# A grouped convolution with two ways of splitting its images: nine of eleven images combined and two by plain taps, instead of three of five combined and two by rows

## The chip, the core and the metric

The kernel runs on one core of one Trainium2 chip. The metric is the device time of one execution in microseconds (us). The core's engines work side by side, each through its own queue in program order: PE (TensorE, matmuls), DVE (VectorE), ACT (ScalarE), POOL (GpSimd), and SP (SyncE), which issues most of the DMA transfers here. They wait for one another by semaphores.

## What is computed

160 images of 128 channels and 32 x 32 pixels are normalised in groups of four channels, convolved 3 x 3 with one of five quantised weight sets, and added to the input:

```python
x = x + _L0_conv_ref(_gn(x), L0_conv_U)

# _gn: per image and group of 4 channels
((g - m) / sqrt(s + eps))

# _L0_conv_ref: U in two quantised parts, then a grouped convolution with N = 5 groups
v1 = s1 * floor(U / s1)
v2 = s2 * floor((U - v1) / s2)
w  = (v1 + v2).reshape(128 * 5, 128, 3, 3)
act = conv(x.reshape(32, 5 * 128, 32, 32), w, stride 1, padding 1, groups 5)
```

Channels lie on the 128 partitions, so one tap of the convolution is a matmul of a 128 x 128 weight matrix with the shifted pixels of an image. The kernel takes the images in an order in which 32 successive ones share a weight set.

## The kernel before

**Numbers in two halves.** [...] each normalised image is split into a high part (the value rounded to 16 bits) and a low part (what is left), and both are multiplied.

**Three ways to do an image.** The two rows of a pair of output rows can share work: with sums and differences of neighbouring lines, the nine taps need fewer products, at the price of additions on DVE.

- *Combined* (`combined(i)` true): high and low parts are both made from sums and differences. `beside_pairs` (POOL, lines 678 and 708) and `combine` (DVE, lines 690 and 697) make the tile `v` of 2048 columns from the raw image; `high_combined` (ACT, line 738) makes `vh`, and `low_combined` (DVE, line 744) makes `vl`. PE does 24 matmuls.
- *By rows* (`combined(i)` false, from image 3 on): the high part `hi` goes through the 18 plain taps (line 788; nine taps, even and odd output rows apart). `low_part` (DVE, line 751) makes the low part, and `combinations` (DVE, lines 764, 772 and 773) makes the tile `rows` of its sums and differences, which PE takes in 12 matmuls (line 843). In all 30. The normalised image `z` comes from POOL (line 714), or from ACT (line 640) where an image is the first of its statistics group (`by_scalar_too`); `hi` comes from ACT (line 648).
- *Plain*: both parts through the taps, 36 matmuls. Only the first three images are done so.

Before the change the pattern is: up to image 6 by rows, then every other image combined, from `FIFTHS` = 30 to `THIRDS` = 130 three of five combined, and then three of four.

**What PE does for an image.** A combined or by-rows image has two products that even and odd output rows share. `sums_of_pairs(i)` puts them in the banks `m2` (one for all images) and `m1a` or `m1b` (by parity of i). ACT copies m2 out (`leave(i)`, line 891), and DVE writes half sum and half difference into the two output banks `eo` of the image (`pairs(i)`, lines 903 and 905). Then `main(i)` adds the rest of the products into these banks. There are two pairs of `eo` banks. When an image is done, ACT copies it out (`residual`, line 929), and POOL issues a DMA that adds it to the output (line 953), where SP has stored the input already (line 968).

**Order.** The order of every queue is the program's own (`tc.manual_schedule()`); nothing reorders it. In iteration i of the main loop, PE does `sums_of_pairs(i + 1)` and then `main(i)`. DVE does, in this order: the low part of image i + 3; a step of the next weight set; `pairs(i + 1)`; in some iterations a scale of the statistics (line 307); `combine(i + 5)`; another weight step; in some iterations five small statistics operations (lines 296 to 302). ACT does: the sum over an image to be measured (line 241, image i + 15); the copy of image i - 1; `leave(i + 1)`; the high part of image i + 4; the squares over the measured image (line 248). POOL does its part of image i + 5 once DVE has come to the low part of the iteration, and then the DMA of image i - 1.

**Weight steps.** A weight set is quantised on DVE and ACT while the set before it is in use. The class `Later` hands out its steps at a pace of 36 over the 25 or so images that remain; `later.take(1)` issues one step if one is due, and two or three places in an iteration ask for one.

**Buffers.** Two images share a chunk of the input. A pool of `CHUNKS` = 11 holds them; after the start, a chunk is loaded (line 497) in the iteration that `consumed` gives for the chunk that lay `CHUNKS` before it. The tiles `vh` rotate through `wide_parts`, with 4 buffers.

Of the kernel before, what the change touches and what calls it, by code (L numbers as in the profile page):

```python
# [10 lines left out]
MM = mybir.dt.float16  # L11
ALU = mybir.AluOpType
# [24 lines left out]
class Later:  # L37
# [25 lines left out]
    def finish(self):  # L63
        run(self.steps)
# [110 lines left out]
def last_of(steps, last=None):  # L175
    for last in steps:
        pass
    return last
# [207 lines left out]
class Main:  # L386
# [24 lines left out]
    STAT_LEAD = 15  # L411
    FURTHER = 11
    LOAD_LEAD = 18
    CHUNKS = 11
    STEADY = 7
    BY_VECTOR = (8, 10, 11, 14, 19, 24, 29, 34)
    FIFTHS = 30
# [10 lines left out]
    def __init__(self, tc, ctx, keep, x, u, out):  # L428
        self.tc = tc
        nc = self.nc = tc.nc  # L430
        self.imgs, C, self.H, self.W = x.shape
        P = self.P = nc.NUM_PARTITIONS
        assert C == P and self.H * self.W == 1024
        self.per_set = self.imgs // N_SETS
        self.xv = x.rearrange("(b n) c h w -> n c b (h w)", n=N_SETS)
        self.ov = out.rearrange("(b n) c h w -> n c b (h w)", n=N_SETS)
        self.uv = u.rearrange("n (o i k) -> n o i k", o=C, k=TAPS)

        def pool(name, bufs, **kw):
            return ctx.enter_context(tc.tile_pool(name=name, bufs=bufs, **kw))  # L440

        self.const = pool("const", 1)
        self.qpool = pool("quant", 1)
        self.wpool = pool("weights", 2)
        self.upool = pool("u", 1)
        self.xpool = pool("x", self.CHUNKS)
        self.zpool = pool("z", 2)
        self.parts = pool("parts", 4)
        self.rows = pool("rows", 5)
        self.wide = pool("wide", 2)  # L450
        self.wide_parts = pool("wide_parts", 4)
        self.evac = pool("evac", 2)
        self.sums = pool("sums", 3)
        self.unread = pool("unread", 1)
        self.small = pool("small", 3)
        self.ps_eo = pool("ps_eo", 2, space=PSUM)
        ps_m = pool("ps_m", 1, space=PSUM)
        ps_small = pool("ps_small", 1, space=PSUM)
        self.steps = Steps(nc, keep)

        self.m1a, self.m1b, self.m2_ps = (
            ps_m.tile([P, self.H // 2, self.W], F32, tag=name, name=name)
            for name in ("m1a", "m1b", "m2")
        )
        self.pair = [self.m1a, self.m2_ps]

        small = ps_small.tile([P, 512], F32, tag="small", name="small")
        self.pt, self.pg = small[:, : ROW * P].rearrange("p (k o) -> p k o", k=ROW), small[:, ROW * P :]
        self.chunks, self.z, self.hi, self.v, self.eo, self.m2 = {}, {}, {}, {}, {}, {}
        self.sum, self.stored = {}, {}  # L470
        self.tables, self.wts, self.across = {}, {}, {}
        self.columns = []

        cuts = [0, 2, 4, 8, 12, 16, 20, *range(24, self.imgs + 1, 8)]
        self.groups = [range(a, b) for a, b in zip(cuts, cuts[1:])]
        self.group_of = {i: k for k, g in enumerate(self.groups) for i in g}
        self.stats = {}
# [173 lines left out]
    def combined(self, i):  # L651

        if i < self.STEADY or i >= self.imgs:
            return False

        if i < self.FIFTHS:
            return i % 2 == 1
        return i % 5 % 2 == 0 if i < self.THIRDS else i % 4 != 2

    def by_scalar_too(self, i):  # L660

# [39 lines left out]
    def beside_pairs(self, i, after):  # L701

        nc = self.nc
        if self.combined(i):
            self.v[i] = self.wide.tile([self.P, 2048], F32, tag="v", name=f"v{i}")
            self.after(self.outer_columns(i), after)
            even, odd = (self.image(i)[:, a::2] for a in range(2))
            ins = nc.gpsimd.tensor_sub(self.v[i][:, 1536:], odd, even)  # L708
        elif self.by_scalar_too(i):
            return  # L710
        else:
            st, j = self.column_of(i)
            z = self.z[i] = self.zpool.tile([self.P, 1024], F32, tag="z", name=f"z{i}")
            ins = nc.gpsimd.tensor_scalar(  # L714
                z, self.image(i), st.ngm[:, j], st.rstd[:, j], ALU.add, ALU.mult
            )
        self.after(ins, after)

    def last_but_one(self, last):
# [28 lines left out]

    def low_part(self, i):
        lo = self.los[i % len(self.los)]  # L750
        self.nc.vector.tensor_sub(  # L751
            lo[:, 1 : self.H + 1, :].rearrange("p h w -> p (h w)"),
            self.z.pop(i),
            self.hi[i].rearrange("p h w -> p (h w)"),
        )
        return lo

    def combinations(self, i):

# [15 lines left out]
    def taps(self, i, part, col, target, parities=(0, 1)):  # L775


        nc, H, W = self.nc, self.H, self.W
        tile, top = part
        n, _ = self.place(i)  # L780
        dw = col - 1
        c0, c1 = max(0, -dw), W - max(0, dw)
        for k in self.KS:
            for a in parities:

                first, end = int(a + k == 0), H // 2 - int(a + k == 3)
                s0 = 2 * first + a + k - 1 + top
                nc.tensor.matmul(  # L788
                    self.bank(target, a)[:, first:end, c0:c1],
                    self.wts[n, col][:, k, :],  # L790
                    tile[:, s0 : s0 + 2 * (end - first) - 1 : 2, c0 + dw : c1 + dw],
                    start=(i < self.FIRST and col == self.COLS[0] and k == 1 and top == 0),
                    stop=False,
                    skip_group_check=True,
                )
# [66 lines left out]
    def conv(self, i, on_the_way):  # L862


        if self.FIRST < i < self.imgs - 1:
            self.sums_of_pairs(i + 1)
        if i == self.FIRST:
            self.main(i, 0)
            self.sums_of_pairs(i + 1)
            on_the_way(self.COLS[1])  # L870
            self.main(i, 1)
            on_the_way(self.COLS[2])
        else:
            self.main(i, 0, lambda: on_the_way(self.COLS[1]))
            self.main(i, 1, lambda: on_the_way(self.COLS[2]))
        del self.v[i]

    def main(self, i, a, between=lambda: None):

        to = self.bank(self.eo[i], a)  # L880
        for step in self.KS:
            if step == self.KS[1] and a == 1 or step == self.KS[2] and a == 0:
                between()
            if not self.combined(i):
                self.taps(i, (self.hi[i], 0), step, self.eo[i], (a,))
            self.product(to, i, a, step, 2 * a)

    def leave(self, i):

# [93 lines left out]
    def run(self):  # L983
        nc, P = self.nc, self.P
# [33 lines left out]
        for k in range(4):  # L1018
            lo = self.const.tile([P, self.H + 2, self.W], MM, tag=f"lo{k}", name=f"lo{k}")
# [95 lines left out]
        for i in range(self.imgs):  # L1115
# [15 lines left out]
            if i < self.FIRST:  # L1131
# [3 lines left out]
                j = (i - 1) % self.FIRST  # L1135
# [10 lines left out]
            else:  # L1146
                j = i - 1
# [35 lines left out]
            else:  # L1183

                last = None
                for k in self.step_of(i, 2):
                    if self.combined(k):
                        last = last_of(self.low_combined(k), last)
                    else:
                        self.low_part(k)  # L1190
                        later.take(1)
                        last = last_of(self.combinations(k), last)
                last = later.take(1, last)
                if last:
                    before = self.last_but_one(last)
# [8 lines left out]
                if i > self.FIRST and not self.by_hand(j):  # L1204
                    self.residual(j)
                    self.accumulate(j)
                if i + 1 < self.imgs:
                    self.leave(i + 1)
                for st in ready:
                    if not st.late:  # L1210
# [1 line left out]
                for k in self.step_of(i, 3):  # L1212
                    if self.combined(k):
                        self.high_combined(k)
                        continue
                    if self.by_scalar_too(k):
                        self.normalise(k)
                    self.high_part(k)
                for k in by_scalar:
                    self.measure(k, (1,))  # L1220
            for st in middle:
# [12 lines left out]

            if i >= self.FIRST:

                if i + 1 < self.imgs:
                    self.pairs(i + 1)
                for st in scaled:
                    st.scales_by_vector()  # L1240
                for k in self.step_of(i, 4):
                    if self.combined(k):
                        self.combine(k)
                    later.take(1)
                later.take_scalar()
                if b in (self.per_set - 4, self.per_set - 2):
                    later.finish()
                for st in ready:
                    if st.late:
                        st.deviations_by_vector()  # L1250
# [65 lines left out]
```

## Time and profile before

| | |
|---|---|
| median of 3 runs | 967.39 us (966.81 to 967.67) |
| the profiled execution | 964.56 us |
| its span, first to last instruction | 962.5 us |
| PE busy | 927.8 us, 96% of the span, 4432 matmuls |
| DVE busy | 902.6 us, 94%, 1269 instructions |
| ACT busy | 862.7 us, 90%, 1167 instructions |
| POOL busy | 460.1 us, 48%, 477 instructions |
| DMA | 254.22 MB, mean 264 GB/s |
| granted clock of PE | 0.995 |

Each engine has its own row, and the rows overlap in time. A busy time is a sum over all stages of the kernel, so it does not tell by itself which engine sets the end. In the lines of a timeline the first number is the start in us from the span's beginning, the second the duration. In the rows of the stretches each engine has its busy time and, in brackets, its instructions. In the rows of waits the numbers are us in total, times, and the longest. Successive matmuls overlap: one lasts about 0.37 us from its start to its end, but the next one starts after some 0.21 us.

### The profile page before, as it was taken

The page shows a single profiled execution, that of the slowest core. Times are in us where ns is not written, and L with a number is a line of the kernel's source. Part 1 is how long each engine was busy: PE and PEld are TensorE (multiplying, and loading weights), DVE is VectorE, ACT ScalarE, POOL GpSimd, SP SyncE. Part 2 cuts the span into 40 slices and gives each one's busy share as a digit, 9 for nine tenths or more (in the row PEclk, how much of TensorE's full clock was granted, in tenths as well). Part 3 has the DMA queues.
Part 4 walks back from the last instruction along what each step waited for, and adds up shares of the span by engine and source line. Part 5 has one row for each costly group of instructions (what it writes and reads, how often), then busy time and mean ns, then how long its engine had stood idle before and what let it go on. Part 6 is the DMA issues. An engine that isn't in the chain of part 4 may idle for free.

```text
span 962.5 us, 13034 instructions
## 1 busy us (share of the span) xinstructions
PE 927.8 (96%) x4432; PEld 433.8 (45%) x4432; DVE 902.6 (94%) x1269; ACT 862.7 (90%) x1167; POOL 460.1 (48%) x477
## 2 busy tenths in 40 slices
PE   2899989999999999999999999999999999999997
PEld 1344434444444444444444444444444444444443
DVE  7989999999899999989999999899999998999993
ACT  5879989999899999999999999999999999997660
POOL 4344434456445445554545445545444366565640
PEclk9999999999999999999999999999999999999999
DMA  9079999999999999999999999999999999856563
GB/s 349 36 267 345 334 348 320 325 321 325 328 321 323 317 295 308 272 306 254 295 251 289 284 293 297 282 277 286 267 273 267 282 279 269 172 91 107 91 107 112
DMA packets 67450, 254.22 MB, mean 264 GB/s; under 512 B 5296, under 2 KB 5296, under 8 KB 67376
## 3 DMA queue, kind: packets, MB, share of 16 engines
q1 hardware_dynamic: 45344, 173.09, 48.0%
q0 software_dynamic: 22032, 80.23, 44.4%
q8 instruction: 36, 0.59, 0.2%
q14 instruction: 38, 0.31, 0.1%
HBM read 89.19 MB, written 164.10 MB: 263 GB/s over the span
## 4 chain that ended last, share of the span: by engine, by line


## 5 line engine op out<-in xcount | busy, mean ns | idle before, releaser
L788 PE MATMUL eo<-hi,wt 128*128 128x496 f16 (+3 forms) x1170 | 310.8, 376 | 2.4 <-DVE eo L905 1.7
L843 PEld LDWEIGHTS <-wt 128*128 128x128 f16 x1884 | 183.9, 99 | 211.5 <-DVE eo L905 2.7
L744 DVE SCALAR_TENSOR_TENSOR vl<-v,rstd,vh 128x2048 f16<-128x2048 f32 x94 | 221.8, 2360 | 0.2 <-ACT vh L738 0.2
L843 PE MATMUL eo<-vh,wt 128*128 128x512 f16 x561 | 210.1, 375 | 1.2 <-DVE eo L905 1.2
L843 PE MATMUL eo<-vl,wt 128*128 128x512 f16 x561 | 210.1, 374 | 0.0
L738 ACT ACTIVATE vh<-v,rstd 128x2048 f16<-128x2048 f32 x94 | 188.2, 2002 | 4.8 <-DVE v L697 4.3
L929 ACT COPY sum<-eo 128x1024 f32<-128x1024 f32 x153 | 161.0, 1052 | 32.3 <-PE eo L843 31.7
L788 PEld LDWEIGHTS <-wt 128*128 128x128 f16 x1242 | 121.2, 99 | 142.8 <-DVE eo L905 4.9
L678 POOL TENSOR_SCALAR v<-xt,ngm 128x64 f32<-128x64 f32 x94 | 79.1, 842 | 202.0 <-DVE vl L744 86.9
L248 ACT ACTIVATE junk<-xt,mv 128x1024 uint8<-128x1024 f32 x152 | 174.4, 1148 | 0.3
L241 ACT ACTIVATE junk<-xt 128x1024 uint8<-128x1024 f32 x152 | 160.5, 1056 | 13.3 <-DMA xt<-in_x_dram 10.0
L714 POOL TENSOR_SCALAR z<-xt,ngm,rstd 128x1024 f32<-128x1024 f32 x49 | 93.3, 1904 | 165.1 <-DVE rows L773 55.0
L843 PEld LDWEIGHTS <-across 128*128 128x128 f16 x1128 | 110.8, 98 | 131.9 <-issue 4.9
L843 PE MATMUL eo<-rows,wt 128*128 128x512 f16 x378 | 143.5, 380 | 0.0
L953 POOL DMA_DIRECT2D out_dram<-sum x153 | 133.7, 874 | 14.4 <-ACT sum L929 6.6
L690 DVE TENSOR_TENSOR v<-xt 128x960 f32<-128x960 f32 x94 | 114.0, 1212 | 0.0
L843 PE MATMUL m<-vl,across 128*128 128x496 f16 (+1 forms) x282 | 106.4, 377 | 2.1 <-DVE vl L744 2.1
L891 ACT ACTIVATE m<-m 128x512 f32<-128x512 f32 x157 | 93.7, 597 | 14.1 <-PE m L843 13.7
L843 PE MATMUL m<-vh,across 128*128 128x496 f16 (+1 forms) x282 | 106.2, 376 | 0.2 <-ACT m L891 0.2
L708 POOL TENSOR_TENSOR v<-xt 128x512 f32<-128x512 f32 x94 | 97.2, 1034 | 0.0
L751 DVE TENSOR_TENSOR lo<-z,hi 128x1024 f16<-128x1024 f32 x66 | 80.6, 1221 | 0.0
L286 POOL TENSOR_TENSOR rstd<-ve,mhalf 128x8 f32<-128x8 f32 (+2 forms) x24 | 42.3, 1761 | 65.1 <-DVE rows L773 21.1
(150 smaller groups left out, 1166.3 us busy)
## 6 DMA issues: line engine op xcount, KB each, us to landing
xt<-in_x_dram SPq DMA_DIRECT2D x78, 1024.0 KB, 9.6
out_dram<-sum POOLq DMA_DIRECT2D x153, 512.0 KB, 8.7
out_dram<-xt SPq DMA_DIRECT2D x76, 1024.0 KB, 14.2
out_dram<-xt SPq DMA_DIRECT2D x7, 512.0 KB, 3.3
u<-in_L_conv_U_dram SPq DMA_DIRECT2D x4, 576.0 KB, 13.6
xt<-in_x_dram SPq DMA_DIRECT2D x4, 512.0 KB, 10.1
range<-in_L_conv_U_dram SPq DMA_DIRECT2D x3, 576.0 KB, 8.3
u<-in_L_conv_U_dram SPq DMA_DIRECT2D x2, 288.0 KB, 3.1
```

Source lines behind the costliest of these rows:

```text
L241: self.nc.scalar.activation(junk, image, ACTF.Copy, scale=-1.0 / image.shape[1], accum_out=self.mv[:, j, 0:1],)
L248: self.nc.scalar.activation(junk, image, ACTF.Square, bias=self.mv[:, j, 0:1], accum_out=self.mv[:, j, 1:2],)
L690: nc.vector.tensor_tensor(self.view(v, 1, (511, 2), (half, H), (1, half - 1)), self.view(x, 1, (1, 2), (W, H), (2, half - 1)), self.view(x ...
L708: ins = nc.gpsimd.tensor_sub(self.v[i][:, 1536:], odd, even)
L714: ins = nc.gpsimd.tensor_scalar(z, self.image(i), st.ngm[:, j], st.rstd[:, j], ALU.add, ALU.mult)
L738: self.nc.scalar.mul(vh, self.v[i], st.rstd[:, j])
L744: yield self.nc.vector.scalar_tensor_tensor(vl, self.v[i], st.rstd[:, j], self.hi[i], ALU.mult, ALU.subtract)
L788: nc.tensor.matmul(self.bank(target, a)[:, first:end, c0:c1], self.wts[n, col][:, k, :], tile[:, s0 : s0 + 2 * (end - first) - 1 : 2, c0 + ...
L843: self.nc.tensor.matmul(out, weights, moving, start=start and j == 0, stop=False, skip_group_check=True)
L891: self.nc.scalar.mul(m2, self.m2_ps, 0.5)
L929: nc.scalar.copy(self.as_banks(i, self.sum[i]), self.flat(i, eo))
L953: added = self.nc.gpsimd.dma_start(self.ov[n, :, b], self.sum.pop(i), accum_op=ALU.add)
```

## The change

From image 30 up to image 129, an image is now combined unless its number leaves the remainder 3 or 8 when divided by 11. Those that are not combined are done plain: both parts go through the 18 taps, without `sums_of_pairs`, `leave`, `pairs` and `combinations`. The first tap of a plain image starts its output bank afresh, and its pair of banks is taken in `main`. POOL makes not only z but also the high part of such an image, from the raw image both times; ACT makes it only where the image is the first of its statistics group. The pool of input chunks has one buffer less, and `wide_parts` has one more.

```diff
-    CHUNKS = 11
+    CHUNKS = 10
...
-        self.wide_parts = pool("wide_parts", 4)
+        self.wide_parts = pool("wide_parts", 5)
...
-        return i % 5 % 2 == 0 if i < self.THIRDS else i % 4 != 2
+        return i % 11 not in (3, 8) if i < self.THIRDS else i % 4 != 2
+
+    def plain(self, i):
+
+        return self.FIFTHS <= i < self.THIRDS and not self.combined(i)
...
                 z, self.image(i), st.ngm[:, j], st.rstd[:, j], ALU.add, ALU.mult
             )
+            if self.plain(i):
+                self.after(ins, after)
+                hi = self.hi[i] = self.parts.tile([self.P, self.H, self.W], MM, tag="hi", name=f"hi{i}")
+                ins = nc.gpsimd.tensor_scalar(
+                    hi.rearrange("p h w -> p (h w)"), self.image(i),
+                    st.ngm[:, j], st.rstd[:, j], ALU.add, ALU.mult,
+                )
...
-                    start=(i < self.FIRST and col == self.COLS[0] and k == 1 and top == 0),
+                    start=((i < self.FIRST or self.plain(i)) and col == self.COLS[0] and k == 1 and top == 0),
...
-        if self.FIRST < i < self.imgs - 1:
+        if self.FIRST < i < self.imgs - 1 and not self.plain(i + 1):
             self.sums_of_pairs(i + 1)
...
+        if self.plain(i) and a == 0:
+            self.eo[i] = self.bank_pair(i)
...
                 self.taps(i, (self.hi[i], 0), step, self.eo[i], (a,))
-            self.product(to, i, a, step, 2 * a)
+            if self.plain(i):
+                self.taps(i, (self.los[i % len(self.los)], 1), step, self.eo[i], (a,))
+            else:
+                self.product(to, i, a, step, 2 * a)
...
-                        self.low_part(k)
+                        last = self.low_part(k) or last
                         later.take(1)
-                        last = last_of(self.combinations(k), last)
+                        if not self.plain(k):
+                            last = last_of(self.combinations(k), last)
...
-                if i + 1 < self.imgs:
+                if i + 1 < self.imgs and not self.plain(i + 1):
                     self.leave(i + 1)
...
-                    self.high_part(k)
+                    if k not in self.hi:
+                        self.high_part(k)
...
-                if i + 1 < self.imgs:
+                if i + 1 < self.imgs and not self.plain(i + 1):
                     self.pairs(i + 1)
```

More of the change, by code (lines that the diff above doesn't have):

```diff
@@ L750, in low_part @@
         lo = self.los[i % len(self.los)]
-        self.nc.vector.tensor_sub(
+        return self.nc.vector.tensor_sub(
             lo[:, 1 : self.H + 1, :].rearrange("p h w -> p (h w)"),
@@ L755, in low_part @@
         )
-        return lo
     def combinations(self, i):
@@ L875, in conv @@
             self.main(i, 1, lambda: on_the_way(self.COLS[2]))
-        del self.v[i]
+        self.v.pop(i, None)
     def main(self, i, a, between=lambda: None):
+        if self.plain(i) and a == 0:
+            self.eo[i] = self.bank_pair(i)
         to = self.bank(self.eo[i], a)
```

## The prediction

> **What bounds the kernel now.** I read the page first (PE, DVE and ACT busy 96, 94 and 90%), then the busy time by stretches. Counting the copies of line 929, which run one image after another, images 30 to 129 fill the span from 226 to 782 us, so I cut that:
>
> ```profile
> core 0: us, PE busy (x) PEld busy (x) DVE busy (x) ACT busy (x) POOL busy (x), PEclk, DMA share, GB/s
> 226.00:400.00 174.00, 173.73 (x837) 81.49 (x836) 166.28 (x230) 168.49 (x232) 83.57 (x80) 1.00 1.04 313
> 400.00:600.00 200.00, 199.53 (x958) 93.41 (x957) 192.22 (x267) 193.32 (x262) 99.36 (x95) 1.00 1.01 281
> 600.00:782.00 182.00, 181.51 (x873) 84.93 (x871) 175.12 (x242) 174.65 (x239) 88.09 (x88) 1.00 1.01 277
> ```
>
> PE is never free at full clock; DVE has 4% and ACT 3.5% to spare, POOL half. The waits of the same stretch show how near DVE is:
>
> ```profile
> DVE eo L903 <- PE m1b L843: 9.1, 8, 2.5
> PE eo L843 <- DVE eo L905: 1.2, 3, 0.5
> ```
>
> Three times PE waited for line 905, the second half of pairs(i), which puts the half sums of image i into its output banks. Since a busy PE hides lost issue time, I measure matmuls from start to start on the timeline:
>
> ```profile
> 422.88 0.38 PE L843 MATMUL eo<-vh,wt 128*128 128x512 f16 x1
> 423.10 0.38 PE L843 MATMUL eo<-vl,wt 128*128 128x512 f16 x1
> 423.16 0.70 DVE L903 SCALAR_TENSOR_TENSOR eo<-m1b,m 128x512 f32<-128x512 f32 x1 [2.53 <-PE m1b L843]
> 423.32 0.37 PE L843 MATMUL eo<-vh,wt 128*128 128x496 f16 x1
> 423.53 0.37 PE L843 MATMUL eo<-vl,wt 128*128 128x496 f16 x1
> 423.89 0.70 DVE L905 SCALAR_TENSOR_TENSOR eo<-m1b,m 128x512 f32<-128x512 f32 x1
> 424.50 1.15 DVE L690 TENSOR_TENSOR v<-xt 128x960 f32<-128x960 f32 x1
> 425.56 0.75 DVE L697 SCALAR_TENSOR_TENSOR v<-xt,twice 128x512 f32<-128x512 f32 x1
> ...
> 437.17 0.81 PE L843 MATMUL m<-rows,wt 128*128 128x512 f16 x3
> 437.82 0.81 PE L843 MATMUL m1a<-rows,wt 128*128 128x512 f16 x3
> 438.47 0.38 PE L843 MATMUL eo<-vh,wt 128*128 128x512 f16 x1
> ...
> 488.22 1.03 POOL L708 TENSOR_TENSOR v<-xt 128x512 f32<-128x512 f32 x1
> 488.29 1.99 DVE L690 TENSOR_TENSOR v<-xt 128x960 f32<-128x960 f32 x1
> 488.56 0.80 PE L788 MATMUL eo<-hi,wt 128*128 128x512 f16 x3
> 491.39 2.34 DVE L744 SCALAR_TENSOR_TENSOR vl<-v,rstd,vh 128x2048 f16<-128x2048 f32 x1
> 493.65 0.55 DVE L145 TENSOR_TENSOR lt<-tt,nnn 128x384 f16<-128x384 f32 x1
> 493.67 0.81 PE L843 MATMUL m<-rows,wt 128*128 128x512 f16 x3
> 494.84 0.70 DVE L905 SCALAR_TENSOR_TENSOR eo<-m1b,m 128x512 f32<-128x512 f32 x1
> 495.60 0.39 PE L843 MATMUL eo<-vh,wt 128*128 128x512 f16 x1 [0.47 <-DVE eo L905]
> ```
>
> To see: a matmul of 512 columns takes 0.216 us, one of 496 contiguous columns 0.209; three by rows take 0.65, so 0.216 each, 31 columns of 32 or not. The main part of a rows image (488.56 to 493.67) takes 5.11 for 18 taps and 6 rows products; less 6 x 0.216 the taps cost 3.81. PE restarts 0.06 us after line 905 ends (495.54 to 495.60), so it waits for both halves. DVE starts pairs 0.28 us after the last half sum has left PE's queue (422.88 to 423.16).
>
> [...] what stands ahead of pairs in DVE's queue delays it, as L744 does at 491.39. [...] L690 takes 1.99 instead of 1.15 us beside POOL's L708, and POOL's L714 runs from 1.2 to 3.2.
>
> **PE, which sets the end.** Of 100 images 60 are combined and 40 by rows now; then 81 combined, 19 plain. Combined: 8 x 0.216 + 16 x 0.209 = 5.07 us. Rows: 3.81 + 12 x 0.216 = 6.40. Plain: twice the taps, 7.62 (low taps not seen in this stretch; same shapes and strides as the high ones, so I take them as equal; 0.01 either way on 342 of them would be 3.4 us either way). Before 60 x 5.07 + 40 x 6.40 = 560.3; after 81 x 5.07 + 19 x 7.62 = 555.6. **Gain 4.7 us**, 12 matmuls fewer. The three waits, 0.5 or 0.6 us each from start to start, belong to places that go: **1.7** more.
>
> **The other queues, from start to start.** DVE loses a rows image's low part, three row sums and pairs (1.14 + 0.60 + 2 x 0.34 + 1.33 = 3.75 us) 40 times, and gains 21 combined (pairs 1.33, L690 1.07, L697 0.66, L744 2.26 = 5.32) and 19 low parts (1.14): -150 + 112 + 22 = -16 us. ACT: 40 x (sum copy 0.96, m2 0.48, hi 0.94) against 21 x (0.96 + 0.48 + 1.89) and 19 x 0.96: -95 + 70 + 18 = -7. POOL gets a second 1.9 us write for 17 images (two are the first of their statistics group and stay ACT's): +32, against 270 idle us; between 1.2 and 3.2 each by row L714, hidden either way: the next image's POOL work is needed by ACT over an iteration later. If that cover went, line 738 would be late and DVE behind it.
>
> SP's queue: with 10 chunks each load waits for a slot freed one chunk later than now. Tightest is images 30 and 31: their load goes out at 104.4, the next one at 111.3, and ACT first reads them near 136.6; landing takes 9.6, so 15 us stay. Stores wait behind loads, but have some 20 images' time. I take zero; bounds 0 to 3 us. A fifth wide_parts buffer removes a wait and costs nothing; it can't lose.
>
> **Where DVE comes late.** Averages improve, but the order gets uneven. Let P be a plain image. Half sums of P don't exist, so between the half sums of P-1 and main(P-1) PE has only main(P-2), 2.54 us, where there were at least 3.8. In DVE's queue the 2.26 us low part of P+1 stands in front of pairs(P-1). From the half sums of P-2: 0.28 + pairs 1.33 + L690 1.07 + L697 0.66 + L744 2.26 + pairs to its end 1.42 + 0.06 = 7.08, in a PE time of 3 x 2.54 = 7.61: spare 0.53. From those of P-3 (adding low part of P, 1.14, pairs 1.33, combine 1.73): 11.28 in 5 x 2.54 = 12.69: spare 1.41. Into this spare fall the steps of the next weight set, 36 / 25 = 1.44 an image at 0.27 to 0.66, and each eighth image's statistics (0.5) and scale (0.4). Walking the pacing of Later through the iterations gives the fillers at every P. Image 47, for one: scale 0.4, steps 0.53 + 0.53 + 0.47 + 0.27 + 0.66 = 2.9, so PE waits 1.4. The others from 36 on: 0.7, 0.2, (1.4), 0.35, 0.65, 0.6, 0.85, 0.4, 0, 0.25, 0.4, 0, 0.8, 0, 0, 1.15, 0.5, 0: **8.2 us**. The same sums for the kernel before leave at least 0.15 of spare everywhere, least at 77 and 117; the trace's waits are at main of 37, 77 and 117, so the method is late by tenths, not early.
>
> Two additions. L690 runs 0.84 long when it follows a scale on DVE and its image is combined (five times in this stretch); that pattern falls into the spare of 47, 63, 102 and 118: 0 to 3.4, I take half, **1.7**. ACT: from main(P-6) on, copies, m2, vh and two measuring passes reach m2 of P-1 some 0.8 before it delays pairs; at 80, where ACT makes both z and hi, 0.6 after: **0.6**. Beyond this bound lies 0 to 3.
>
> Sum: -4.7 - 1.7 + 8.2 + 1.7 + 0.6 = **+4.1 us**. The profiled execution took 964.56 us (962.5 of span and 2.1 around it), 2.8 below the median of 967.39; the stage's differences don't depend on that, so I add to the median: 971.5.
>
> **Rivals.**
> - The PE gain comes through (faster). If DVE's steps fall into its waits, or the low part of P+1 starts early enough, only -4.7 - 1.7 = -6.4 stays: 961.0. For it: DVE has 16 us less to do and ACT 7. Against: DVE can't do pairs in advance. It decides where PE waits less than 0.34 us (6.4 / 19) per plain image on average.
> - Half the waits: at 0.34 they cancel, 967.4.
> - ACT becomes the bound in the runs of five: 5.53 us an image from start to start (copy 0.96, m2 0.48, vh 1.89, passes 1.06 + 1.13) against PE's 5.07. Its lag of 0.46 x 5 = 2.3 is within the slack of some 3 that the m2 bank gives; if it were not, 0.5 at each of nine longer gaps adds 4.5: 976.
> - Loads late: 3 us more, 974.5, ACT waiting for DMA before 230 us.
> - The change not doing what it says: the remainders 3 and 8 of 11 occur 9 and 10 times from 30 to 129, so the counts are as said; no chance.
>
> **How the numbers follow.** A measurement tells about 0.2% (1.9 us) from no change. DVE late as summed, 0.52; ACT or loads on top, 0.08; cancelling, 0.16; the PE gain, 0.24. Waits from 4 (fillers shorter by 0.3 at each P) to 16 (0.2 longer, L690 long at all four, ACT at its bound) give -2.4 to +9.6; the range goes down to most of the PE gain: 962.5 to 976.
>
> **What would show it.** Right: 12 matmuls fewer; PE waiting for line 905 ten times or more, some 10 us in all, at main(P-1), after L744; DVE busy down by some 20, POOL up by some 30. Wrong: PE waits for 905 below 3 us and the stage ends near 776 (step of the spare), waits for m2 or sum copies (ACT), or "junk from xt by DMA" before 230 us (loads).

## The result and the profile after

| | before | after |
|---|---|---|
| median of 5 runs | 966.90 us (965.58 to 967.67) | **989.45 us** (988.61 to 991.14) |
| ratio, 95% interval | | 1.0236 [1.0222, 1.025] |
| span of the profiled execution | 962.5 us | 986.9 us |
| granted clock of PE | 0.995 | 0.992 |

The kernel became 22.6 us slower; 4.1 were forecast. The direction and the place of most of PE's waits are the predicted ones. The size is not, and most of what made it has no term in the forecast.

First the part of the page with the busy times, and of its costliest groups the two of DVE that grew most (busy us, mean ns of one, idle before):

```profile
PE 930.1 (94%) x4420; PEld 432.1 (44%) x4420; DVE 916.3 (93%) x1150; ACT 857.7 (87%) x1128; POOL 480.7 (49%) x518
...
L755 DVE SCALAR_TENSOR_TENSOR vl<-v,rstd,vh 128x2048 f16<-128x2048 f32 x115 | 275.1, 2392 | 0.2 <-ACT vh L749 0.2
...
L694 DVE TENSOR_TENSOR v<-xt 128x960 f32<-128x960 f32 x115 | 155.6, 1353 | 5.9 <-POOL v L682 5.9
```

The same two in the kernel before, where they are lines 744 and 690 (groups by line):

```profile
L744 DVE SCALAR_TENSOR_TENSOR vl<-v,rstd,vh 128x2048 f16<-128x2048 f32 x94 | 221.8, 2360 | 0.2 <-ACT vh L738 0.2
L690 DVE TENSOR_TENSOR v<-xt 128x960 f32<-128x960 f32 x94 | 114.0, 1212 | 0.0
```

Twelve matmuls fewer, as counted, and the plain image 30 takes PE 7.62 us, as priced. But DVE's busy time went up by 13.7 us, from 902.6, where it was to fall by some 20. Line 694 is 141 ns longer on average and now waits for POOL's line 682; line 755 is 32 ns longer.

Counted from the last matmuls back, image 129 ends at 818 us. Before, it ended at 795, not at 782 as the prediction has it: its window up to 782, and the one up to 803 used here, both end at image 127. PE has no wait between these points and the end of image 129 in either kernel, so the sums of waits are not touched. The busy times by stretch:

```profile
core 0: us, PE busy (x) PEld busy (x) DVE busy (x) ACT busy (x) POOL busy (x), PEclk, DMA share, GB/s
226.00:400.00 174.00, 165.30 (x779) 76.32 (x778) 162.31 (x183) 158.45 (x206) 87.38 (x90) 0.98 1.01 284
400.00:600.00 200.00, 193.44 (x931) 90.03 (x929) 189.14 (x216) 185.16 (x243) 101.78 (x106) 1.00 0.99 272
600.00:803.00 203.00, 196.14 (x935) 91.18 (x933) 193.70 (x220) 188.33 (x248) 102.11 (x106) 0.99 0.99 267
```

PE, which was never free here, now is for 22 of 577 us, and in two stretches its granted clock is below 1.00 (0.98 and 0.99). Of the rows of waits from 226 to 803 us (total, times, longest), these five say for whom PE waits, and for whom DVE does:

```profile
PE eo L853 <- DVE eo L920: 20.9, 13, 3.6
DVE eo L918 <- PE m1a L853: 8.1, 6, 2.6
DVE eo L918 <- PE m1b L853: 7.0, 7, 1.8
DVE rstd L307 <- POOL rstd L286: 6.2, 10, 1.6
DVE v L694 <- POOL v L682: 5.4, 15, 0.5
```

Line 920 is the second half of pairs (905 before). PE's row was 1.2 us in three places. From start to start all of PE's waits add up to 24.8 us, where the kernel before has 1.7; two of them, 1.5 us together, are for DVE's small operations (at lines 273 and 558), not for pairs. In the whole kernel line 694 was long, near 1.98 us, 6 times; now it is 26 times.

The longest stands at main(57), ahead of plain image 58. The timeline around it, queues of DVE, POOL and PE merged:

```profile
340.28 0.70 DVE L918 SCALAR_TENSOR_TENSOR eo<-m1b,m 128x512 f32<-128x512 f32 x1 [1.59 <-PE m1b L853]
...
357.36 2.04 POOL L286 TENSOR_TENSOR rstd<-ve,mhalf 128x8 f32<-128x8 f32 x1 [3.28 <-DVE vl L755]
...
359.44 0.37 DVE L307 TENSOR_SCALAR rstd<-rstd,lift 128x8 f32<-128x8 f32 x1 [1.57 <-POOL rstd L286]
...
385.78 2.35 DVE L755 SCALAR_TENSOR_TENSOR vl<-v,rstd,vh 128x2048 f16<-128x2048 f32 x1
388.04 0.55 DVE L145 TENSOR_TENSOR lt<-tt,nnn 128x384 f16<-128x384 f32 x1
388.51 0.69 DVE L918 SCALAR_TENSOR_TENSOR eo<-m1b,m 128x512 f32<-128x512 f32 x1
389.24 0.70 DVE L920 SCALAR_TENSOR_TENSOR eo<-m1b,m 128x512 f32<-128x512 f32 x1
390.00 0.39 PE L853 MATMUL eo<-vh,wt 128*128 128x512 f16 x1 [3.61 <-DVE eo L920]
...
391.58 2.34 DVE L755 SCALAR_TENSOR_TENSOR vl<-v,rstd,vh 128x2048 f16<-128x2048 f32 x1
391.73 0.63 PE L853 MATMUL eo<-vh,wt 128*128 128x512 f16 x1
392.15 0.63 PE L853 MATMUL eo<-vl,wt 128*128 128x512 f16 x1
...
393.84 0.35 DVE L146 TENSOR_TENSOR k<-nnn,lt 128x384 f16<-128x384 int16 x1
394.03 0.41 POOL L682 TENSOR_SCALAR v<-xt,ngm 128x64 f32<-128x64 f32 x1 [3.37 <-DVE vl L755]
394.40 1.03 POOL L712 TENSOR_TENSOR v<-xt 128x512 f32<-128x512 f32 x1
394.47 1.98 DVE L694 TENSOR_TENSOR v<-xt 128x960 f32<-128x960 f32 x1 [0.28 <-POOL v L682]
```

To see: (1) The pairs at 388.51 stand behind the low part at 385.78 and a weight step, as predicted. (2) Between 359.44 and 388.51, 29 us and five iterations, DVE has no idle time at all, and its last idle time was a wait for POOL. The last time that it waited for PE's half sums, and so was on time, was at 340.28. (3) After the wait, matmuls start 0.42 us apart instead of 0.21. (4) In the iteration of image 57 nothing lies between the low part (391.58) and the combination but a short weight step; POOL's line 712 then runs beside line 694, which takes 1.98 us instead of 1.15. The iteration around 359.44 is of the same kind, the one ahead of plain image 52: with no pairs in between, DVE comes to its scale (line 307) while POOL is still at the power that the scale needs (line 286), and waits 1.57 us. That happens three times; in the kernel before no such wait is longer than 0.2 us.

### The profile page after: what moved, and what is told of

It reads as the page before. It is cut to its first block, busy times and chain, and to the rows that moved or that the text cites. A ratio compares the mean times of both kernels' runs of the same rounds, so it can differ in the third digit from the quotient of the medians.

```text
span 986.9 us, 12896 instructions
## 1 busy us (share of the span) xinstructions
PE 930.1 (94%) x4420; PEld 432.1 (44%) x4420; DVE 916.3 (93%) x1150; ACT 857.7 (87%) x1128; POOL 480.7 (49%) x518
## 4 chain that ended last, share of the span: by engine, by line
## 5 line engine op out<-in xcount | busy, mean ns | idle before, releaser
L853 PE MATMUL eo<-vh,wt 128*128 128x496 f16 (+1 forms) x687 | 260.2, 379 | 21.5 <-DVE eo L920 21.4
L755 DVE SCALAR_TENSOR_TENSOR vl<-v,rstd,vh 128x2048 f16<-128x2048 f32 x115 | 275.1, 2392 | 0.2 <-ACT vh L749 0.2
L853 PE MATMUL eo<-vl,wt 128*128 128x496 f16 (+1 forms) x687 | 259.9, 378 | 0.0
L749 ACT ACTIVATE vh<-v,rstd 128x2048 f16<-128x2048 f32 x115 | 230.2, 2001 | 14.8 <-DVE v L701 14.3
L798 PE MATMUL eo<-hi,wt 128*128 128x496 f16 (+3 forms) x792 | 209.7, 375 | 2.6 <-DVE eo L920 1.7
L241 ACT ACTIVATE junk<-xt 128x1024 uint8<-128x1024 f32 x152 | 160.4, 1056 | 14.0 <-DMA xt<-in_x_dram 10.6
L694 DVE TENSOR_TENSOR v<-xt 128x960 f32<-128x960 f32 x115 | 155.6, 1353 | 5.9 <-POOL v L682 5.9
L853 PE MATMUL m<-vl,across 128*128 128x512 f16 x345 | 129.5, 375 | 2.4 <-DVE vl L755 2.4
L853 PE MATMUL m<-vh,across 128*128 128x512 f16 x345 | 129.5, 375 | 0.3 <-ACT m L906 0.3
L798 PE MATMUL eo<-lo,wt 128*128 128x496 f16 (+1 forms) x378 | 99.5, 375 | 0.0
L701 DVE SCALAR_TENSOR_TENSOR v<-xt,twice 128x512 f32<-128x512 f32 x115 | 85.5, 744 | 0.0
L853 PE MATMUL m1b<-vl,across 128*128 128x496 f16 (+1 forms) x204 | 77.2, 378 | 0.0
```

The costliest lines, as they stand in the source:

```text
L241: self.nc.scalar.activation(junk, image, ACTF.Copy, scale=-1.0 / image.shape[1], accum_out=self.mv[:, j, 0:1],)
L694: nc.vector.tensor_tensor(self.view(v, 1, (511, 2), (half, H), (1, half - 1)), self.view(x, 1, (1, 2), (W, H), (2, half - 1)), self.view(x ...
L701: nc.vector.scalar_tensor_tensor(v[:, 1024:1536], even, st.twice[:, j], odd, ALU.add, ALU.add)
L749: self.nc.scalar.mul(vh, self.v[i], st.rstd[:, j])
L755: yield self.nc.vector.scalar_tensor_tensor(vl, self.v[i], st.rstd[:, j], self.hi[i], ALU.mult, ALU.subtract)
L798: nc.tensor.matmul(self.bank(target, a)[:, first:end, c0:c1], self.wts[n, col][:, k, :], tile[:, s0 : s0 + 2 * (end - first) - 1 : 2, c0 + ...
```

## The experiments

What was to be told apart, with the letters by which expectations call some of it: the **order** in DVE's queue, the low part of P+1 ahead of pairs(P-1) (A); **POOL beside DVE** in the iteration of P-1 (B); POOL's **second write** for a plain image, `hi`, which delays what POOL does next (D); DVE's work as a whole, weight steps included; and the loads (C). From e3 on the expectations use B in a wider sense as well: DVE is short of time, whatever the reason. Each edit is to the kernel after, unless said otherwise, and is shown shortened. PE's waits are given from start to start within the stage, "half rate" is the time lost in matmuls 0.42 us apart instead of 0.21. Ratios are to the kernel before, measured beside each run at 966.4 to 967.0 us; "less than after" compares medians taken at different times, so half a us of it means nothing.

### e1: the buffers alone

On the kernel before:

```
-CHUNKS = 11
+CHUNKS = 10
-self.wide_parts = pool("wide_parts", 4)
+self.wide_parts = pool("wide_parts", 5)
```

> The kernel before with only the two buffer sizes of the change: 10 input chunks and 5 wide_parts. Theory A (PE waits for pairs in front of plain images cause the loss): no difference, within 2 us of the kernel before. Rival C (later loads): 3 us or more slower, ACT waiting for input transfers before 230 us.

Measured: 967.1 against 966.57 us, ratio 1.0005 [0.9998, 1.0012]. One chunk less and one wide buffer more cost nothing. Loads are out as a cause.

### e2: POOL's part kept away from DVE's combination

```
-self.beside_pairs(k, before)
+if not (self.plain(i + 1) and self.combined(k)):
+    self.beside_pairs(k, before)
...
-self.combine(k)
+if self.plain(i + 1):                 # in iteration P-1
+    ...
+    self.beside_pairs(k, self.combine(k).ins)
+else:
+    self.combine(k)
```

> The changed kernel, but in the iteration before a plain image, where no pairs stand between DVE's low part and its combine, POOL makes its part of v after DVE's combine instead of beside it. Theory B (DVE loses its spare to POOL: L694 runs 0.84 us long some 20 times and waits for L682): the long L694 at the plain images go, DVE's waits for POOL too, PE waits fall from 25 us to the forecast 10 or so, the throttled stretches behind the longest waits go, 970 to 975 us. Theory A alone (the order of low part and pairs, whatever POOL does): 985 us or more.

Measured: 997.35 us, ratio 1.0321 [1.0303, 1.0338]. Slower than after by 7.9 us, where B expected a gain; A's range, 985 us or more, includes it, but neither expected a loss. DVE's busy time did fall by 9 us, to 907.2, but POOL's part is now so late that ACT waits for it; the waits of e2:

```profile
ACT vh L750 <- POOL v L713: 40.9, 18, 4.4
...
PE eo L854 <- DVE eo L921: 22.7, 17, 2.9
```

The edit put a new wait in the place of the old one, so it says nothing on A or B.

### e3: pairs(P-1) ahead of the low part of P+1

```
+first = self.plain(i + 2) and i > self.FIRST
+if first:
+    self.measure(k, (0,)); self.residual(j); self.leave(i + 1); self.pairs(i + 1)
 ...                                   # low part of i + 3, first weight step
-    self.pairs(i + 1)
+    self.pairs(i + 1)                 # only if not first
```

> The changed kernel, but in the iteration two before a plain image P DVE does pairs(P-1) ahead of the low part of P+1 (with ACT's copy of m2 in front of it as before). Theory A: the low part is due 2.54 us later than pairs, so each wait shortens by up to 2.5 us; PE waits fall from 25 us to 2 to 5, 963 to 968 us. Theory B without A: DVE is short of time as a whole in the runs, the wait only moves to the half sums of P+1 for vl; 980 us or more.

Measured: 1020.31 us, ratio 1.056 [1.0542, 1.0578]: 31 us slower than after. The expectation of A fell. The groups of e3 show what the swap did:

```profile
L694 DVE TENSOR_TENSOR v<-xt 128x960 f32<-128x960 f32 x115 | 171.1, 1487 | 12.2 <-POOL v L682 12.2
```

Now pairs no longer lie between low part and combination in the iteration of P-2 either, so line 694 meets POOL twice per plain image: 134 ns more on average, and 12 us of waiting for POOL. ACT's high part waits longer for DVE's combination (64 us in all, 14 in the kernel after). PE still waits for pairs (23.2 us), and not for the low part as B had it. Pairs between low part and combination are what keeps the two engines apart. That the order is the fault is not disproved; this way of changing it is.

### e4: the half sums moved instead of the pairs

PE makes the half sums of P+1 ahead of main(P-1), so that DVE gets pairs(P+1) and pairs(P-1) further from PE's need; m1a and m1b alternate over the images that have half sums.

```
-return self.m1b if i % 2 else self.m1a
+return self.m1b if (i - sum(self.plain(k) for k in range(i))) % 2 else self.m1a
...
-if self.FIRST < i < self.imgs - 1 and not self.plain(i + 1):
-    self.sums_of_pairs(i + 1)
+if self.FIRST < i < self.imgs - 1 and not self.plain(i):
+    self.sums_of_pairs(i + 2 if self.plain(i + 1) else i + 1)
```

> The changed kernel, but PE does the half sums of P+1 before main(P-1) instead of after it, with m1a and m1b alternating over the images that have half sums. Theory A: pairs(P-1) has 5 instead of 2.5 us, vl of P+1 is due when pairs was; spare grows by about 1.9 us, PE waits fall from 25 to some 6 us, 965 to 970 us. Theory B without A: 980 us or more, PE waiting for vl.

Measured: 979.71 us, ratio 1.0135 [1.0118, 1.0152], 9.7 less than after, and so between the two expectations. PE's waits fell from 24.8 to 20.2 us and the half rate from 4.8 to 0.3 (granted clock over the run 0.995 instead of 0.992). The waits of e4, 226 to 800 us:

```profile
PE m L853 <- DVE vl L755: 11.5, 11, 2.7
...
PE eo L853 <- DVE eo L920: 3.4, 6, 1.0
```

Most of the time PE now waits for the low part itself, not for pairs: with pairs out of the way, DVE is still late. The order is part of the loss, a shortage on DVE the larger part.

### e5 and e6: no weight steps, after and before

Weight steps are left out; all images use the weights of the first set.

```
-if n + 1 < N_SETS:
+if n + 1 < 1:
...
-n, _ = self.place(i)
+n = 0
```

> The changed kernel without the weight steps: sets 2 to 5 are not quantised on DVE and ACT nor turned on PE, and all images use the first set's weights. Theory B (DVE is short of time in the runs of combined images): DVE gets some 20 us per set back, PE waits in the stage fall from 25 us to under 5, and it ends 4 to 6 us below the kernel before without its weight steps. Theory A with fixed order alone: the waits stay at 15 us or more, 10 us above it.

> The kernel before, without the weight steps in the same way. PE is its bound from image 30 on, so only the stage before that, where DVE has no time to spare, gets shorter: 950 to 962 us by both theories. It is what the changed kernel without weight steps is compared with.

Measured: e5 952.61 us, e6 956.59 (ratios to the kernel before 0.9857 [0.984, 0.9874] and 0.9902 [0.9885, 0.992]). With DVE freer in both, by 79 us and 69 us of busy time, the change is a **gain of 4.0 us**, near the 4.7 worked out for PE. The waits of e5, 226 to 800 us:

```profile
DVE eo L918 <- PE m1a L853: 23.1, 21, 3.2
DVE eo L918 <- PE m1b L853: 22.5, 20, 2.5
```

DVE waits for PE 41 times there, and PE for DVE 0.6 us in all, though line 694 is as long as in the kernel after (mean 1353 ns). So the loss is made in DVE's time: the same order, the same long line 694 and the same buffers cost next to nothing once DVE has time to spare. The weight steps also took 18 us of ACT's busy time (857.7 to 839.6); that ACT's time is not what counts is seen in e8, where ACT does 13 us more and the kernel is faster.

### e7: POOL without its computed part for images P+4

POOL writes zeros in place of its two parts of `v` for the images that are combined in the iteration of P-1.

```
+if self.plain(i - 4):
+    ...                               # memset to 0.0: the outer columns, and
+    ...                               # self.v[i][:, 1536:]
+    return
```

> The changed kernel, but for the images P+4, whose combine on DVE follows the low part without pairs between, POOL writes zeros in place of its two computed parts of v; these parts are left out. Theory B: the long L694 of these iterations go (18 x 0.84 us and the waits for L682), PE waits fall from 25 to some 10 us, 968 to 976 us. Theory A alone: 985 us or more. If L694 stays long beside the zeros, it tells nothing.

Measured: 978.89 us, ratio 1.0126 [1.0108, 1.0145], 10.6 less than after, 3 us above B's range and below A's. The group of line 694 in e7:

```profile
L694 DVE TENSOR_TENSOR v<-xt 128x960 f32<-128x960 f32 x115 | 138.3, 1203 | 1.9 <-POOL v L712 1.8
```

The lengthening is gone (1203 ns; before the change 1212), and waits of 17.3 and half rate of 1.7 us remain (granted clock 0.996). POOL beside line 694 is a cause, of some 10 us, and not the only one.

### e8: `hi` of plain images by ACT

```
-if self.plain(i):
+if False:                             # in beside_pairs: hi is ACT's
```

> The changed kernel, but ACT makes the high part of all plain images, as it does for images by rows, and POOL only z. Theory D (POOL's second write holds up the power behind it, and DVE waits 1.6 us for rstd in the runs before images 41, 58 and 129): these three waits go, 3 to 6 us less, 983 to 986 us. Against it: ACT has 17 x 0.94 = 16 us more to do; if ACT becomes late, 990 us or more.

Measured: 982.54 us, ratio 1.0166 [1.0141, 1.019], 6.9 less than after. But not by D's mechanism. The group of line 755 and, over the whole run, the wait for POOL's power in e8 (6.5 us in the kernel after):

```profile
L755 DVE SCALAR_TENSOR_TENSOR vl<-v,rstd,vh 128x2048 f16<-128x2048 f32 x115 | 271.0, 2357 | 0.2 <-ACT vh L749 0.2
```

```profile
DVE rstd L307 <- POOL rstd L286: 6.3, 10, 1.6
```

The scale waits as long as ever. What changed is the length of DVE's instructions: line 755 is back at its old mean (2357 ns; 2360 before, 2392 after), and so are the weight steps: line 143 at 613 instead of 666 ns, line 145 at 559 instead of 618, line 162 at 741 instead of 791, each the value of the kernel before. DVE's summed durations fell by 11.5 us, PE's waits to 18.8. POOL's second write costs time because DVE's instructions beside it get longer. One of the 17 writes in the kernel after, queues merged:

```profile
333.89 0.70 DVE L920 SCALAR_TENSOR_TENSOR eo<-m1a,m 128x512 f32<-128x512 f32 x1
334.31 1.18 POOL L724 TENSOR_SCALAR hi<-xt,ngm,rstd 128x1024 f16<-128x1024 f32 x1
334.49 1.40 DVE L143 SCALAR_TENSOR_TENSOR tt<-nnn,s2nlo,tt 128x384 f32<-128x384 int16 x1
```

Line 143 takes 0.61 us elsewhere. Beside these writes six executions of line 755 take 3.0 us in the mean instead of 2.36, and the weight steps there some 0.8 us more; the pairs (lines 918 and 920) stay at 0.70.

### e9: e4 and e8 together

> Two of the tried edits together on the changed kernel: half sums of P+1 ahead of main(P-1), and ACT making the high part of plain images. If both work on one shortage of DVE time, and alone gave 9.8 and 6.9 us less, together they give less than the 16.7 us of their sum but more than either: 973 to 978 us. If they were independent: 973 or less.

Measured: 969.94 us, ratio 1.0034 [1.0022, 1.0045]. That is 19.5 us less than after, where the single gains, 9.7 and 6.9, add up to 16.6: outside the first expectation, and in the range given for independent effects. The 2.9 us between them are not clear of the four runs' intervals. PE's waits are 10.1 us.

### e10: DVE makes POOL's part of images P+4

```
 def outer_columns(self, i, engine=None):
...
+if self.plain(i - 4):                 # in combine
+    self.outer_columns(i, nc.vector)
+    nc.vector.tensor_sub(v[:, 1536:], odd, even)
...
+    if self.plain(i - 4):             # in beside_pairs
+        return
```

> The changed kernel, but DVE itself makes POOL's two parts of v for the images P+4, behind its combine, so that POOL is not at work beside it there; nothing is left out. It costs DVE some 0.8 us at 18 places and saves the 0.84 us of the long L694 and up to 0.5 of waiting for L682. Theory B in its strict form (only DVE's time counts): about even to 5 us better, 984 to 990 us. If POOL's load itself matters more (late rstd, late v), 975 to 983 us.

Measured: 984.16 us, ratio 1.0187 [1.0167, 1.0208]. Even though DVE gets work on top, 38 instructions, its busy time is 3.3 us lower (913.0) and the kernel 5.3 us faster than after, at the low end of B's range.

### e11: e4, e8 and e10 together

> The three edits together (half sums early, high part by ACT, POOL's parts of the images P+4 by DVE). By theory B DVE's spare decides: 967 to 975 us; below 965 only if every wait of PE goes and the gain of 12 fewer matmuls comes through.

Measured: 965.48 us, ratio 0.9987 [0.998, 0.9994], 1.5 us below the expected range. PE's waits are 5.5 us from start to start; by its rows of waits 3.6 are for the low part, 0.7 for DVE ahead of the turning of a weight set (line 558), none for pairs.

### e12: e11 with two weight steps held back

In an iteration with the low part of a plain image no weight step is issued ahead of pairs.

```
-later.take(1)
+if not self.plain(k):
+    later.take(1)
-last = later.take(1, last)
+if not self.plain(i + 3):
+    last = later.take(1, last)
```

> The three edits together, and in the iteration whose low part is that of a plain image DVE takes no weight step ahead of pairs (the steps come later; one place behind combine stays). By theory B the last waits (PE for vl of P+1, some 5 us) shrink by up to 0.5 us at each of ten places: 961 to 965 us, below both kernels. If the steps only move into the next tight place: 965 us or more.

Measured: 964.84 us, ratio 0.9978 [0.9969, 0.9986]: 24.6 less than after, just inside the expected range, and **faster than the kernel before** by 2.15 us, 0.2%: little, but the interval lies below 1. All waits of PE in e12 from 226 to 790 us:

```profile
PE m L858 <- DVE vl L760: 1.8, 4, 0.9
PE small L558 <- DVE ngm L298: 0.9, 1, 0.9
PE eo L858 <- DVE eo L925: 0.4, 1, 0.4
```

and the group of line 694, whose wait for POOL is gone too:

```profile
L694 DVE TENSOR_TENSOR v<-xt 128x960 f32<-128x960 f32 x115 | 140.4, 1220 | 0.4 <-DVE rstd L307 0.2
```

## Why the prediction was right and wrong

**The sum, term by term**, from the profiled execution, but for the first row, which compares the medians of e5 and e6 (in e5 PE still waits 0.6 us):

| term | forecast us | measured us |
|---|---|---|
| PE has 12 matmuls less to do | -4.7 | -4.0 (e5 against e6) |
| old waits go | -1.7 | -1.7 |
| PE waits for DVE and ACT (8.2 + 1.7 + 0.6) | +10.5 | +24.8 |
| PE at half rate after waits | none | +4.8 |
| sum | +4.1 | +23.9; the span grew by 24.4 |

**Right.** The matmuls by count. PE waiting for the second half of pairs(P-1) behind the low part, "ten times or more". ACT not the bound, its busy time down by 5.0 us. Loads and buffers at nothing (e1). POOL up, by 20.6 us instead of 32 (17 writes of 1.18 us, priced at 1.9). And the rival of the PE gain was placed correctly: it comes through where DVE's waits go (e5, nearly e12).

**Wrong, first: "DVE -150 + 112 + 22 = -16 us".** The count of instructions is right, but each was priced at its duration before. With the means of before, the summed durations would have fallen by 22.0 us; they rose by 4.3. (In the traces the next DVE instruction often starts before the last has ended, as at 388.04 above, so summed durations are larger than busy time.) The difference, 26.3, is stretching: 115 x 141 ns = 16.2 on line 694, 115 x 32 ns = 3.7 on line 755, and the remaining 6.4 mostly on weight steps. The prediction saw line 690's long form (1.99 us) and even its neighbour on POOL, but read it as a matter of scales, four places, 1.7 us. It did not ask what had kept the two apart elsewhere: pairs, which the change takes out of 19 iterations. The same pairs had given POOL time for its power, so the three waits of 1.6 us at line 307 are theirs too. Beside the POOL write it set only a bound on POOL ("hidden either way"), not what that write does to DVE. e7 and e8 show both to be real, by taking each away: 10.6 and 6.9 us.

**Wrong, second: the walk "from the half sums of P-2" and "of P-3".** It took DVE to start each chain on time. Its own numbers speak against that: a combined image takes 5.32 us of DVE against PE's 5.07, with nothing for weight steps. So along a run of combined images DVE falls back, and only the plain image gives time back. By the stretches above, DVE is busy 545 of 577 us after the change, and PE's own matmuls (577 less 24.8 of waits and 4.8 at half rate) take 547; before, DVE was busy 534 of 556. On average DVE has next to nothing left to catch up with.

The trace shows when DVE was last on time: when it last waited for PE's half sums or for ACT's copy of m2. Where that is at most four images back and no long line 694 lies in between, the forecasts hold within 0.4 us: at plain images 36, 52, 63, 69, 96, 124 and 129, as 0.42 against 0.7 at 36 and 0.71 against 0.85 at 69. At 47 and 102 it is four images back too, but with a long line 694: 2.81 against 1.4 and 2.22 against 0.8. (The prediction's first addition allowed for half of 0.84 us at such a place.) Where it is 8 to 26 images back, the forecasts are mostly too low: 3.77 against 0.65 at 58 (the timeline above), 2.34 against 0.2 at 41, 1.86 against 0.4 at 74, 0.63 against 0 at 80, 2.9 against 0.4 at 91, 1.38 against 0 at 113 and 2.78 against 1.15 at 118; only at 85 and 107 did they hold. The two errors feed each other: longer instructions lengthen the chains.

**Wrong, third: no term for PE's clock.** After three of the waits, of 2.65, 3.61 and 2.62 us, PE ran some 3.2 us at half rate (matmuls 0.42 us apart instead of 0.21) and lost 1.6 each time. The granted clock was 0.50 for 3.41 us each time, from 322.8, 391.1 and 742.7 us. The trace of the kernel before shows such stretches too, from 40.9 and 129.7 us, outside the stage that the prediction cut out. How long a wait has to be for it, these traces don't settle: in the kernel after, 2.62 us ahead of 743 us were followed by it, while 2.75 ahead of 583 and 2.06 ahead of 648 were not (granted clock 1.00 in the 3.4 us after each). So from its length alone it could not be foreseen for a single wait.

**Open.** How much of the 26 us of stretching, of the waits for POOL's line 682 and power, and of the run's length each makes in PE's waits can't be told, since they act on the same chain. B by itself was tried only through e7 and e10, which also change the work of POOL or DVE; e2 was confounded. What e12 gains is accounted for: its waits from start to start are 4.4 us up to 803 us and its half rate 0.3 (granted clock 0.997), so -4.7 - 1.7 + 4.4 + 0.3 = -1.7, against -2.15 measured.

## What to carry to other kernels

Where an engine's instructions get longer beside another's, as DVE's line 694 did beside POOL's line 712 (1.98 us instead of 1.15), the price of an instruction is that of its neighbourhood: before an instruction between two others is removed, ask which pair on other engines it has kept apart. Carry lateness on from one iteration to the next: compare, over each run of like iterations, what the second engine needs with what the first gives it, and only reset where the trace shows it waiting for the first. A long wait on PE can cost more than itself: three of fifteen did here, 1.6 us each.

## What the runs showed of the hardware that was not expected

- DVE's subtraction of 128x960 f32 (line 694) takes 1.15 us alone. Beside POOL's subtraction of 128x512 f32 (line 712), which itself stays at 1.03, it took 1.98 to 2.00 us in 26 of 44 places of the kernel after, and 1.15 to 1.26 in the other 18.
- DVE's instructions get longer beside POOL's write of `hi` (1.18 us) too: a weight step of line 143 takes 1.40 us instead of 0.61, line 755 3.0 instead of 2.36, while the pairs stay at 0.70.
- PE ran at half rate (granted clock 0.50, matmuls 0.42 us apart instead of 0.21) for some 3 us after waits of 2.62, 2.65 and 3.61 us in the kernel after, but not after one of 2.75.
